# First scans of a Mamba and attention kernel: delta-times-u loads moved to SyncE's queue, the u piece loaded later

## The chip, the cores and the metric

The kernel runs on one core of a Trainium2 chip. The metric is the device time of one execution in microseconds (us); lower is better. Times of the kernel before are the median of three runs; the profile is of one more execution of the same program. TensorE is PE in the profile, VectorE DVE, ScalarE ACT, GpSimd POOL and SyncE SP.

## What is computed

The input x has 4 images of 4096 tokens (64 by 64) with 128 channels. Layer 0 adds to x the sum of three selective scans (forward, backward, and over 16 interleaved slices) of the normalised image; layer 1 adds attention and then a layer of 64 experts. The change concerns the scans alone. For each of the three orders the reference does this, with 256 channels d and 16 states n:

```python
def step(h, inp):
    u_, de_, b_, c_ = inp
    dA = jnp.exp(de_[..., None] * A)
    h = h * dA + (de_ * u_)[..., None] * b_[:, None, :]
    y = jnp.einsum('bdn,bn->bd', h, c_)
    return (h, y)
...
y = y + Dp[None, :, None] * x      # x is u here
return y * silu(z)
```

u is a convolved and activated projection of the image, delta (de_ above) a softplus of a further projection, and b_ and c_ are rows of another projection (B and C in the kernel).

## The kernel before

**Inputs and scans.** Class Inputs makes u, delta, delta times u (called du), B and C for every image, order and chunk of 1024 tokens, and keeps them in HBM. Its matmuls are lines L416 (the convolution, cv), L431 (xd), L444 (dt) and L375 (the gate z); ScalarE activates their results (u L423, r L449, z L381) and issues the stores of u and delta at L400, of B and C at L435 and L436, and of the gate at L383. Class Scans runs the recurrences.

**A step of a scan.** One step handles 8 channels by 16 states, or rather half of the states of 16 channels, on 128 partitions and 1024 tokens: a tile of delta and a tile of du, each 16 rows spread over 8 partitions a row (512 KB written), serve two steps. There are 3 orders x 4 chunks x 32 steps = 384 steps for an image. The steps of a group of four give 32 channels of y. For image 0 (alone is true) a step is:

- ScalarE: dA = exp(delta times A), L546, in place for odd steps, into another tile for even ones;
- VectorE: dB = du times B into PSUM, L555, then the scan h, L565, which goes on from the column ends of the chunk before;
- GpSimd: the last column of h is kept in ends, L567, and hC = h times C, L572;
- TensorE: sums hC over states into y, L603, for two steps at a time, one group later; after the fourth step of a group it adds the D term at L608 as a matmul of a diagonal (ScalarE makes it at L613) with the piece of u;
- ScalarE copies y to o, L628; SyncE stores o two steps later, as one DMA (L641, order 0) or four (L648, L652, orders 1 and 2).

**Order of the work.** The order is written out by hand (manual_schedule): every engine does its instructions in the order in which the program names them, and a DMA is issued by the sequencer of the engine that it is called on, in that engine's order. In the first phase the loop of tile_kernel gives the generator of image 0's scans one turn and the generators of the inputs of all four images 1.4 turns, alternately; the scans' loop has two turns a step. So on ScalarE the exponentials stand between the activations of the inputs, and on TensorE the y matmuls between those of the inputs.

**Loads.** At the start of step s the loop calls load(s + ahead), where ahead is 4 for image 0. For even steps it loads delta (3 buffers, issued by SyncE) and du (4 buffers, issued by ScalarE when alone, otherwise by SyncE), both at L531. For the first step of a group it also loads the piece of u for the D term, 128 KB, at L536 (3 buffers, SyncE). At the first two steps of a chunk, load first brings rows of B and C (L512). The piece of u is read at L608, in the third step of the following group. After its loads, step s calls exp(s + 3), then the y matmuls of the turn, then step(s), which does the scan and the next dB.

Of the kernel before, what the change touches and what calls it, by code (L numbers as in the profile page):

```python
# [11 lines left out]
F32 = mybir.dt.float32  # L12
# [4 lines left out]
P = 128  # L17
# [9 lines left out]
T = 1024  # L27
NC = L // T
NS2 = NS // 2
# [182 lines left out]
def orders(b):  # L212

    return ORDERS[min(b, 1)]
# [253 lines left out]
class Scans:  # L468
# [24 lines left out]
    def of_image(self, b, made, alone=False):  # L493

        nc = self.nc
# [5 lines left out]
        steps = [(order, c, k, j) for order in orders(b) for c in range(NC) for k in range(8) for j in range(4)]  # L501
        spread, ends, tiles, stores = {}, {}, {}, []
        ahead = 2 * self.AHEAD if alone else self.AHEAD

        def rows_of(order, c, q):
            for i, name in enumerate(("B", "C")):
                if alone and 2 * (c % 2) + q == 3:
                    t = self.lone.tile([P, T], F32, tag=name, name=f"{name}{q}_{b}_{order}_{c}")
                else:
                    t = self.rows.tile([P, T], F32, tag=name, bufs=3, name=f"{name}{q}_{b}_{order}_{c}")  # L510
                src = made[b, order, c]["bc"][i, q * NS2 : (q + 1) * NS2]
                nc.sync.dma_start(out=t, in_=src.unsqueeze(0).to_broadcast([16, NS2, T]))  # L512
                spread[order, c, name, q] = t
            if q == 1:
                return
            if c < NC - 1:
                ends[order, c] = self.small.tile([P, NB], F32, tag="ends", name=f"ends_{b}_{order}_{c}")

        def load(s):

            order, c, k, j = steps[s]
            if k == 0 and j < 2:
                rows_of(order, c, j)
            if j % 2:
                return
            at = 8 * (4 * k + j)
            for name, bufs in (("delta", 3), ("du", 4)):
                t = self.deep.tile([P, T], F32, tag=name, bufs=bufs, name=f"{name}_{b}_{s}")
                src = made[b, order, c][name][at : at + 16]
                by = nc.scalar if alone and name == "du" else nc.sync  # L530
                by.dma_start(out=t, in_=src.unsqueeze(1).to_broadcast([16, NS2, T]))  # L531
                tiles[name, s] = tiles[name, s + 1] = t
            if j == 0:
                u = self.rows.tile([P, T // 4], F32, tag="u", bufs=3, name=f"us_{b}_{s}")
                src = made[b, order, c]["u"][32 * k : 32 * k + 32]
                nc.sync.dma_start(out=u, in_=src.rearrange("p (g t) -> g p t", g=4))  # L536
                tiles["u", s] = u

        def exp(s):
            order, c, k, j = steps[s]  # L540
            t = tiles["delta", s]
            if j % 2 == 0:
                tag, bufs = ("dB", 3) if alone else ("dA", 2)
                tiles["delta", s] = self.deep.tile([P, T], F32, tag=tag, bufs=bufs, name=f"dA_{b}_{s}")
            A = self.ws[order]["A"][:, j % 2, 2 * k + j // 2].unsqueeze(1)
            nc.scalar.activation(tiles["delta", s], t, AF.Exp, scale=A)  # L546
# [10 lines left out]
        def step(s):  # L557

            order, c, k, j = steps[s]
            at = 4 * k + j  # L560
            dA, dB = tiles.pop(("delta", s)), tiles["du", s]
            tag = "dA" if alone and j % 2 else "h"
            h = self.deep.tile([P, T], F32, tag=tag, bufs=2, name=f"h_{b}_{s}")
            first = 0.0 if c == 0 else ends[order, c - 1][:, at : at + 1]
            nc.vector.tensor_tensor_scan(h, dA, dB, first, ALU.mult, ALU.add)  # L565
            if c < NC - 1:
                nc.gpsimd.tensor_copy(ends[order, c][:, at : at + 1], h[:, T - 1 :])  # L567
            if alone:
                if s + 1 < n:
                    inputs(s + 1)  # L570
                tiles["du", s] = self.lone.tile([P, T], F32, tag="hC", bufs=6, name=f"hC_{b}_{s}")
                nc.gpsimd.tensor_mul(tiles["du", s], h, spread[order, c, "C", j % 2])  # L572
                return
            if s + 1 < n:
                inputs(s + 1)
            nc.vector.tensor_mul(dB, h, spread[order, c, "C", j % 2])  # L576
            product(s)
# [32 lines left out]
        def diagonal(s):  # L610
            order, c, k, j = steps[s]
            d = self.lone.tile([P, P], F32, tag="diagonal", name=f"diag_{b}_{s}")
            nc.scalar.mul(d, self.ident, self.ws[order]["D"][:, k : k + 1])  # L613
            tiles["D", s] = d
# [44 lines left out]
        def have(s):  # L659
            while (b,) + steps[s][:2] not in made:  # L660
                yield

        for s in range(ahead):
            yield from have(s)
            load(s)
# [10 lines left out]
        def sums(s):  # L676

            if s % 4 in (1, 2):
                first = s // 4 * 4 - 4 + (0 if s % 4 == 1 else 2)
                total(first, y)  # L680
                total(first + 1, y)

        def finish(s, y):
            out(s, y)
            self.bank.leave()

        for s in range(n):
            if s + ahead < n:
                yield from have(s + ahead)
            turn = s % 4 if s >= 4 else None  # L690
            if turn == 1:
                while not self.bank.free:
                    self.did.add("wait")
                    yield
                y = self.bank.grab(f"y_{b}_{s}")
                if alone:
                    diagonal(s - 2)
            if s + ahead < n:
                load(s + ahead)
            if s + further < n:  # L700
                exp(s + further)
                self.did.add("exp")
            if turn in (1, 2):
                sums(s)
                self.did.add("sum")
            yield
            step(s)
            if turn == 2 and not alone:
                finish(s - 3, y)
            if turn == 0 and alone and s >= 8:  # L710
                finish(s - 5, y)
            if turn == 2 and stores:
                stores.pop()()
            yield
            self.steps[b] += 1
# [975 lines left out]
```

## Time and profile before

| | |
|---|---|
| median of 3 runs | 11474.27 us (11466.94 to 11487.52) |
| the profiled execution, its own time | 11464.56 us |
| span of that execution, first to last instruction | 11462.8 us |
| TensorE busy, share of the span | 87% |
| ScalarE busy | 88% |
| VectorE busy | 72% |
| GpSimd busy | 33% |
| DMA from SyncE's queue | 1345.93 MB, 44.5% of 16 engines' time |
| DMA from ScalarE's queue | 233.46 MB, 6.7% |
| scans of image 0 | first scan at 108 us, last ends near 1863 us |
| between 90 and 1870 us | VectorE busy 1494.0 us, TensorE 1362.0, GpSimd 1304.6, ScalarE 1151.3; DMA 0.80 busy, 223 GB/s |

In the views, a line such as "L546 ACT ACTIVATE dA<-delta,A" names the line of the program, the engine, the operation and what it writes and reads. A row of waits reads: who waited, for whom, us in total, number of times, the longest. A row of the order of time reads: start, duration (both us), engine, line, operation, count, and in brackets the idle time before it with what ended it. "ACTq" and "SPq" are the sequencers of ScalarE and SyncE issuing DMAs. In the name delta<-d_delta, d_ marks the tensor in HBM.

### The profile page before, as it was taken

How to read it: one execution, taken by the hardware profiler on the slowest of the kernel's cores; microseconds unless marked ns; L12 is line 12 of the kernel's file. 1: busy time of each engine (PE TensorE's matmuls, PEld its weight loads, DVE VectorE, ACT ScalarE, POOL GpSimd, SP SyncE). 2: the span in 40 equal slices, each digit the busy share in tenths (PEclk: the TensorE clock that was granted, in tenths of full speed). 3: DMA queues.
4: the chain of work that ended last, by engine and by line, in shares of the span. 5: the costliest groups of instructions: out<-in, count | busy, mean ns of one | idle time of the engine just before them, and what ended most of it. 6: DMA issues, size and time to landing. Idle time of an engine off the chain costs nothing.

```text
span 11462.8 us, 183364 instructions
## 1 busy us (share of the span) xinstructions
PE 9939.9 (87%) x68550; PEld 3315.0 (29%) x68550; DVE 8234.0 (72%) x8300; ACT 10070.4 (88%) x11032; POOL 3749.5 (33%) x3891
## 2 busy tenths in 40 slices
PE   6687783688998889999998898999998999999995
PEld 2233332222222222222222222222222223333323
DVE  6988877788888987999888979988998321111212
ACT  4666663799999999999999999999999999989992
POOL 5867764332323312424333224233332110000000
PEclk9888886899999999999999999999999999999997
DMA  6877877555565665655556656655556332222225
GB/s 196 237 228 219 221 206 211 159 149 148 148 160 151 168 176 155 160 149 149 147 145 157 195 154 156 160 141 147 150 146 168 118 98 71 74 73 83 75 65 185
DMA packets 900979, 1747.52 MB, mean 152 GB/s; under 512 B 203150, under 2 KB 443846, under 8 KB 899830
## 3 DMA queue, kind: packets, MB, share of 16 engines
q1 hardware_dynamic: 731198, 1345.93, 44.5%
q10 hardware_dynamic: 75032, 233.46, 6.7%
q0 software_dynamic: 93856, 156.41, 4.8%
q8 instruction: 538, 8.81, 0.3%
q14 instruction: 355, 2.91, 0.1%
HBM read 1379.76 MB, written 355.47 MB: 151 GB/s over the span
## 4 chain that ended last, share of the span: by engine, by line
PE 39%; ACT 25%; issue 14%; DVE 11%; DMA 7%; POOL 2%; SPq 1%; ACTq 1%; DVEq 0%; POOLq 0%
PE acc L1031 21%; ACT e L1022 20%; PE s L1017 10%; DVE h L565 5%; PE cv L416 4%; DMA delta<-d_delta 2%; DMA du<-d_du 2%; DVE dB L555 1%; ACT dA L546 1%; PE y L603 1%; POOL hC L572 1%; ACT delta L546 1%; PE fo L1188 1%; PE h L1175 1%; POOL ends L567 1%
## 5 line engine op out<-in xcount | busy, mean ns | idle before, releaser
L1022 ACT ACTIVATE e<-s 128x1024 f32<-128x1024 f32 x8192 | 7779.8, 1107 | 235.6 <-PE s L1017 219.7
L1031 PE MATMUL acc<-e,val 128*32 128x512 f32 x32768 | 5248.4, 615 | 105.8 <-ACT av L1040 92.7
L1017 PE MATMUL s<-qm,key 32*128 32x512 f32 x16384 | 2650.9, 501 | 591.2 <-ACT e L1022 561.3
L1017 PEld LDWEIGHTS s<-qm,key 32*128 32x128 f32 x16384 | 1012.7, 184 | 4449.5 <-issue 2485.0
L567 POOL COPY ends<-h 128x1 f32<-128x1 f32 x1152 | 1277.0, 1111 | 2352.7 <-DVE h L565 2338.6
L555 DVE TENSOR_TENSOR dB<-du,B 128x1024 f32<-128x1024 f32 x960 | 1231.8, 1283 | 484.5 <-DMA du<-d_du 251.1
L565 DVE TENSOR_TENSOR_SCAN h<-dA,ends,dB 128x1024 f32<-128x1024 f32 x576 | 1350.3, 2344 | 142.7 <-ACT dA L546 102.3
L1031 PEld LDWEIGHTS acc<-e,val 128*32 128x32 f32 x32768 | 970.2, 109 | 1605.1 <-issue 785.7
L546 ACT ACTIVATE dA<-delta,A 128x1024 f32<-128x1024 f32 x768 | 936.1, 1219 | 275.3 <-DMA delta<-d_delta 244.6
L565 DVE TENSOR_TENSOR_SCAN h<-delta,ends,du 128x1024 f32<-128x1024 f32 x432 | 1012.3, 2343 | 128.2 <-ACT delta L546 64.1
L572 POOL TENSOR_TENSOR hC<-h,C 128x1024 f32<-128x1024 f32 x384 | 1008.2, 2626 | 257.8 <-PE y L603 187.3
L546 ACT ACTIVATE delta<-delta,A 128x1024 f32<-128x1024 f32 x768 | 938.2, 1222 | 56.6 <-issue 22.3
L576 DVE TENSOR_TENSOR du<-h,C 128x1024 f32<-128x1024 f32 x576 | 701.1, 1217 | 0.1
L576 DVE TENSOR_TENSOR dB<-h,C 128x1024 f32<-128x1024 f32 x576 | 701.0, 1217 | 0.0
L555 DVE TENSOR_TENSOR du<-du,B 128x1024 f32<-128x1024 f32 x576 | 690.5, 1199 | 3.7 <-DMA B<-d_bc 3.7
L1046 POOL DMA_DIRECT2D d_ctx<-av x512 | 261.2, 520 | 1019.5 <-DVE av L1040 644.3
L416 PE MATMUL cv<-xn,conv 128*128 128x512 f32 x1024 | 478.9, 623 | 22.4 <-ACT xn L349 14.1
L597 POOL DMA_DIRECT2D d_du<-x_delta x272 | 157.7, 580 | 1003.0 <-DVE x_delta L596 940.8
L565 DVE TENSOR_TENSOR_SCAN h<-dA,dB 128x1024 f32<-128x1024 f32 x192 | 438.7, 2285 | 60.7 <-ACT dA L546 46.7
L603 PE MATMUL y<-hC,sel 128*32 128x256 f32 x3072 | 259.7, 472 | 248.1 <-issue 100.4
L603 PE MATMUL y<-dB,sel 128*32 128x256 f32 x4608 | 377.1, 399 | 9.7 <-DVE xT L1215 5.4
L565 DVE TENSOR_TENSOR_SCAN h<-delta,ends,dB 128x1024 f32<-128x1024 f32 x144 | 337.6, 2344 | 58.2 <-ACT delta L546 44.2
(252 smaller groups left out, 7338.1 us busy)
## 6 DMA issues: line engine op xcount, KB each, us to landing
delta<-d_delta SPq DMA_DIRECT2D x768, 512.0 KB
du<-d_du SPq DMA_DIRECT2D x576, 512.0 KB
du<-d_du ACTq DMA_DIRECT2D x192, 512.0 KB
key<-d_q SPq DMA_DIRECT2D x352, 256.0 KB
d_u<-u ACTq DMA_DIRECT2D x48, 1024.0 KB
d_delta<-r ACTq DMA_DIRECT2D x48, 1024.0 KB
B<-d_bc SPq DMA_DIRECT2D x96, 512.0 KB
C<-d_bc SPq DMA_DIRECT2D x96, 512.0 KB
```

Source lines behind the costliest of these rows:

```text
L416: nc.tensor.matmul(banks[2 * m + g], w["conv"][:, k, m * P : (m + 1) * P], reads(k, g), start=(k == 0), stop=(k == 3))
L546: nc.scalar.activation(tiles["delta", s], t, AF.Exp, scale=A)
L555: nc.vector.tensor_mul(tiles["du", s], du, spread[order, c, "B", j % 2])
L565: nc.vector.tensor_tensor_scan(h, dA, dB, first, ALU.mult, ALU.add)
L567: nc.gpsimd.tensor_copy(ends[order, c][:, at : at + 1], h[:, T - 1 :])
L572: nc.gpsimd.tensor_mul(tiles["du", s], h, spread[order, c, "C", j % 2])
L576: nc.vector.tensor_mul(dB, h, spread[order, c, "C", j % 2])
L603: nc.tensor.matmul(y[32 * g : 32 * g + 32, : T // 4], self.sel[:, j // 2, :], hC[:, 256 * g : 256 * g + 256], start=(j == 0), stop=(j == 3 ...
L1017: nc.tensor.matmul(s_ps[:, k, :], keys[f"{i // 4}"][rows, cut].bitcast(F32R), queries[j, qb][rows, :].bitcast(F32R), start=True, stop=True,)
L1022: nc.scalar.activation(e, s_ps, AF.Exp, scale=1.0 / math.sqrt(D))
L1031: nc.tensor.matmul(accs[j, qb][32 * k : 32 * k + 32, :], v[:, k * VW : k * VW + 32], es[i][k // 2][:, k % 2, :], start=(kc == 0), stop=(kc ...
L1046: nc.gpsimd.dma_start(out=self.context[b][h * D : h * D + D, cut], in_=av[32 * k : 32 * k + D, :])
```

## The change

For image 0, the loads of du are issued by SyncE, directly after those of delta. The piece of u is no longer loaded with the loads of the first step of its group, four steps ahead; a function of its own, bring_u, loads it in the second step of its own group, after that step's loads. For the other images the piece is loaded where it was. The loads themselves, their shapes and the numbers of buffers are the same.

```diff
             for name, bufs in (("delta", 3), ("du", 4)):
                 t = self.deep.tile([P, T], F32, tag=name, bufs=bufs, name=f"{name}_{b}_{s}")
                 src = made[b, order, c][name][at : at + 16]
-                by = nc.scalar if alone and name == "du" else nc.sync
-                by.dma_start(out=t, in_=src.unsqueeze(1).to_broadcast([16, NS2, T]))
+                nc.sync.dma_start(out=t, in_=src.unsqueeze(1).to_broadcast([16, NS2, T]))
                 tiles[name, s] = tiles[name, s + 1] = t
-            if j == 0:
-                u = self.rows.tile([P, T // 4], F32, tag="u", bufs=3, name=f"us_{b}_{s}")
-                src = made[b, order, c]["u"][32 * k : 32 * k + 32]
-                nc.sync.dma_start(out=u, in_=src.rearrange("p (g t) -> g p t", g=4))
-                tiles["u", s] = u
+            if j == 0 and not alone:
+                bring_u(s)
+
+        def bring_u(s):
+            order, c, k, j = steps[s]
+            u = self.rows.tile([P, T // 4], F32, tag="u", bufs=3, name=f"us_{b}_{s}")
+            src = made[b, order, c]["u"][32 * k : 32 * k + 32]
+            nc.sync.dma_start(out=u, in_=src.rearrange("p (g t) -> g p t", g=4))
+            tiles["u", s] = u
...
             if s + ahead < n:
                 load(s + ahead)
+            if alone and s % 4 == 1:
+                bring_u(s - 1)
             if s + further < n:
                 exp(s + further)
                 self.did.add("exp")
```

## The prediction

> **What bounds the kernel now.** The page was read first for where the time lies (span 11462.8 us; the chain gives TensorE 39% and ScalarE 25%, nearly all of it in the attention loop after 2200 us). The change touches only the scans of image 0, so the second view is the table of stretches, one for each chunk of 32 steps. Columns: stretch, length, busy time (and instructions) of TensorE, its weight loads, VectorE, ScalarE, GpSimd, then granted clock, DMA share, GB/s.
>
> ```profile
> core 0: us, PE busy (x) PEld busy (x) DVE busy (x) ACT busy (x) POOL busy (x), PEclk, DMA share, GB/s
> 382.00:515.00 133.00, 92.48 (x446) 38.46 (x444) 124.55 (x74) 81.80 (x102) 118.45 (x67) 0.86 0.92 265
> 652.00:811.00 159.00, 136.65 (x512) 54.13 (x511) 121.65 (x64) 114.79 (x135) 106.04 (x66) 0.88 0.75 223
> 811.00:962.00 151.00, 117.53 (x522) 50.14 (x520) 121.84 (x71) 98.89 (x125) 107.90 (x66) 0.87 0.82 227
> 1566.00:1733.00 167.00, 153.34 (x562) 62.69 (x560) 124.53 (x66) 114.78 (x139) 104.50 (x64) 0.90 0.78 213
> ```
>
> VectorE needs 120 to 125 us for a chunk; the first four take 133 to 137, the later ones up to 167. So VectorE sets the pace of the early chunks, and later something makes it wait. The third view is VectorE's list of waits from 90 to 1870 us (total, times, longest), with the one row of SyncE's list and the group row for its multiply in the same stretch:
>
> ```profile
> DVE dB L555 <- DMA du<-d_du: 83.3, 45, 7.3
> DVE h L565 <- ACT dA L546: 62.5, 20, 10.6
> DVE h L565 <- ACT delta L546: 52.0, 28, 4.9
> ```
>
> ```profile
> SPq L536 <- PE y L608: 219.7, 54, 10.4
> ```
>
> ```profile
> L555 DVE TENSOR_TENSOR dB<-du,B 128x1024 f32<-128x1024 f32 x384 | 536.4, 1397 | 95.2 <-DMA du<-d_du 83.3 <-DMA B<-d_bc 0.3
> ```
>
> VectorE waits 83 us for du and 114 us for ScalarE's exponentials. The multiply's mean is 1397 ns where an unhindered one takes 1233: 384 x 0.164 = 63 us more. The fourth view, the order of time around one such wait, says why du is late:
>
> ```profile
> 1485.03 0.51 SPq L531 DMA_DIRECT2D delta<-d_delta  x1
> ```
>
> ```profile
> 1486.71 2.42 ACT L449 ACTIVATE r<-dt,dt_proj_b 128x512 f32<-128x512 f32 x4
> 1489.16 0.38 ACTq L400 DMA_DIRECT2D d_delta<-r  x1
> ...
> 1495.65 2.06 ACT L381 ACTIVATE z<-z 128x512 f32<-128x512 f32 x4
> 1497.75 0.38 ACTq L383 DMA_DIRECT2D d_sz<-z  x1
> 1498.22 0.71 ACTq L531 DMA_DIRECT2D du<-d_du  x1
> ```
>
> ```profile
> 1508.14 1.23 DVE L555 TENSOR_TENSOR dB<-du,B 128x1024 f32<-128x1024 f32 x1 [4.24 <-DMA du<-d_du]
> ```
>
> delta and du of step 310 belong together; SyncE issued delta at 1485.03, ScalarE came to du at 1498.22, 13.2 us later, behind its activations and behind a 1 MB store in its own queue. Pairing all 192 issues in order, du is issued a median of 6.7 us after its delta, over 10 us in 60 of them, and earlier in 28.
>
> **What the Trainium skill says.** "DMA: Bandwidth & Descriptors", section Issuing engines are not separate DMA queues: DMAs of all issuing engines run on the same 16 engines and interleave, so a second issuer saves only issue time. The trace agrees that engines are shared: from 1019 to 1024 us ScalarE's queue moved 1.54 MB and SyncE's 0.00, though a delta was issued at 1020.0. The same page, section Anatomy of one DMA: a wait stands at the issuing sequencer, ahead of dispatch. The trace agrees: the du above was not even issued. "SBUF — State Buffer", section SBUF: two separate sides: VectorE with two SBUF inputs and a GpSimd op that reads SBUF exclude each other for a whole instruction. The trace fits: after a du wait the multiply often takes 2.4 to 3.4 us, as if it waited out a 2.35 us hC of GpSimd.
>
> **The change, part by part.**
> 1. *du issued on SyncE (192 issues).* A new delta's buffer is released by the scan five steps before its own; SyncE issues it 0.03 us after that scan ends in three cases of four. du follows 0.55 us later (one issue is 0.53). It needs no other buffer wait: its buffer was last read three steps earlier than delta's. From there to its multiply are four steps of 3.75 us (1497.80 to 1501.55, scan to scan), less the 0.55: 14.4 us. Two loads of 0.52 MB at the 223 GB/s of this stretch are 4.7 us, after some 1.5 us in which nothing moves yet (a delta issued at 1005.02 found the engines idle; bytes move from 1006.5). In all 44 du waits after the first step, du had been issued 4.5 to 14.5 us before the multiply, delta 16.4 to 26.7 us. I take these waits as gone: 76.2 us, and the 33.8 us by which the multiplies right after them were stretched: 110.0 us freed on VectorE.
> 2. *What of this is kept.* ScalarE's exponentials are next late. I count a freed wait as kept only as far as ScalarE, before the next scan that waited for an exponential, itself waited for delta or for VectorE; there it moves along. That leaves 69.5 of the 110.0: 41.8 in the eight chunks where TensorE is busy under 80%, 27.7 in the four (652, 1109, 1406 and 1566 us on) where it is busy 85 to 92%. In those I keep a third, 9, since cv matmuls hold ScalarE (168 us of waits in 69 places) and, through y, GpSimd (187 us in 57). Kept: 51 us. Bounds: 17.5 (the first four chunks alone, where no exponential is late) and 110.
> 3. *ScalarE rid of the issues.* 192 x 0.57 us = 109 us of its in-order time. Counting only issues that lie between ScalarE's last wait of any kind and a late exponential, and no more than that wait's length, 24.6 us of 119 us come free; most of it is in the four full chunks, so I take half, 12. Bounds 0 and 38 (the sum when waits for TensorE are not counted as breaks).
> 4. *SyncE gains 192 x 0.53 = 102 us of issuing.* Its work per four steps of 15 us is then four loads, one u and up to four stores, under 5 us. The cover is its own waiting for scans (666 us in its list). It passes the stores of o, which wait for ScalarE, and B and C loads: du is now held behind these as delta already is; delta was held up 78.6 us in 31 places, 7.7 at most, against 14.4 us of room. Nothing on average, up to the price in the third rival.
> 5. *The u piece.* Moved from ten steps before its D matmul to five; SyncE's 219.7 us of waiting for that matmul goes, because the buffer of three groups earlier has then long been read. It stood behind delta in front of the next load, which waits for a scan anyway, so I count nothing; bound: part of those 78.6 us. The new lead is some 17 us (four steps, and hC's 2.35) against 1.5 + 5 us to land behind delta and du (1.18 MB), 11.5 if a store holds the engines 5 us. At the 11 chunk starts, behind B and C, I charge 0.5 us each: 5 us.
>
> Sum: 51 + 12 - 5 = 58 us. The profiled execution took 11464.6 us (span and 1.8 around it), so 11406.6; the median of before is 11474.3, 9.7 above it, so **11416** for a median. Image 0's result is what attention waits for, and nothing after 1900 us is changed, so what the scans gain the end gains.
>
> **The rivals.**
> *TensorE and GpSimd take over the waits.* Over 650 to 1100 us the chain gives PE cv 32.9%, GpSimd's hC and ends 19.8% and du only 2.4%; GpSimd needs 2.35 + 1.24 us a step, nearly VectorE's 3.75, and cannot catch up. Then only the 17.5 us of the early chunks remain: 11457. Against it: du waits also lie where TensorE is under 80% busy.
> *All of it is kept:* 110 + 38 = 148 us, 11326, should exponentials move along, since delta no longer shares the engines with a du from the other queue. ScalarE waits 174 us for delta. Against it: the full chunks.
> *SyncE's queue as a single file (slower).* At a chunk start it gets B, C, delta, du twice within 8 us: eight loads, 4.2 MB. At 223 GB/s a load is 2.35 us, so the first du lands 9.4 + 1.5 us after the first load is issued, 9.3 after its own issue, and the second 10.9 us after its own. If ScalarE's d_u and d_delta, 2.1 MB, take the engines first, as one did at 1019, at that stretch's 310 GB/s for 6.8 us, these become 16.1 and 17.7, past the 14.4 us of room from which it decides. Price: 1.7 + 3.3 us late and twice 2.4 of stretch, 9.8 us, at 11 starts 108; less the 58 gained elsewhere: 50 slower, 11524. Against it: the bytes are the same as before on the same engines, and the stretch with 265 GB/s has hardly a wait.
>
> **Chances.** Forecast 0.50 (its own range 11385 to 11448), takeover 0.18, all kept 0.20, single file 0.12. About 0.2%, 23 us, is what a measurement can tell from no change. Faster 0.70, same 0.18, slower 0.12. The range 11330 to 11485 leaves out just under half of "all kept" and most of "single file".
>
> **What would show it.** Right: du rows of SyncE 0.5 us behind delta's; VectorE's du waits under 20 us; the multiply's mean near 1300 ns; SyncE's L536 row gone; ScalarE's row in VectorE's waits not above 150 us; last scan near 1805 us. Wrong: exponential or GpSimd waits grow by what du's lost, or du waits gather at chunk starts.

## The result, and the profile after

The changed kernel takes 11448.0 us (median of 11 runs, 11436.9 to 11458.3) against 11476.9 (11 runs, 11466.9 to 11491.0): a ratio of 0.9973 with an interval of 0.9963 to 0.9982, or 29 us less. The forecast was 58.

The profiled execution took 11451.7 us (span 11450.0). The last scan of image 0 ends at 1835 us instead of 1863, and the first score matmul of attention starts at 2078 instead of 2106. These 28 us agree with the 29 between the medians. The two profiled spans differ by 12.8 only: what follows the last scan is the same work in both, and took 9600 us in the one execution and 9615 in the other (9596 to 9619 in e1 to e3 below). The runs of one kernel spread over 21 to 24 us.

First the table of stretches, one for each chunk of 32 steps, as before (stretch, length, busy time of TensorE, its weight loads, VectorE, ScalarE, GpSimd, clock, DMA share, GB/s):

```profile
core 0: us, PE busy (x) PEld busy (x) DVE busy (x) ACT busy (x) POOL busy (x), PEclk, DMA share, GB/s
373.00:505.00 132.00, 95.64 (x462) 40.14 (x451) 126.23 (x75) 83.77 (x105) 118.99 (x67) 0.85 0.89 263
643.00:794.00 151.00, 133.23 (x515) 53.79 (x514) 117.58 (x64) 114.56 (x135) 110.48 (x66) 0.92 0.78 235
794.00:943.00 149.00, 114.39 (x523) 49.40 (x521) 126.84 (x70) 99.22 (x125) 110.69 (x67) 0.89 0.83 230
1540.00:1697.00 157.00, 143.89 (x538) 59.05 (x537) 125.74 (x65) 112.88 (x137) 105.68 (x63) 0.92 0.77 218
```

The same four chunks took 133, 159, 151 and 167 us; the first four together went from 544 to 538 us, the last eight from 1211 to 1191. So most of the gain lies in the late chunks. Each of these figures is of one execution: e2 below, as fast as the kernel before, took 550 and 1221, so differences of up to some 10 us between such figures show nothing. Next VectorE's waits from 90 to 1870 us, the row of its multiply there, and SyncE's longest wait:

```profile
DVE h L568 <- ACT dA L549: 81.8, 26, 10.9
DVE h L568 <- ACT delta L549: 59.0, 24, 6.4
DVE dB L558 <- DMA du<-d_du: 30.7, 4, 14.9
```

```profile
L558 DVE TENSOR_TENSOR dB<-du,B 128x1024 f32<-128x1024 f32 x385 | 551.8, 1433 | 43.8 <-DMA du<-d_du 30.7
```

```profile
SPq L530 <- DVE h L568: 737.0, 153, 11.1
```

Of the du waits of 83 us, 31 are left, and these are at the start of the scans (13.6), at one place in the fourth chunk (2.3), and for the next image's first load at the end of the stretch. The waits for exponentials went from 114 to 141 us, and the multiply's mean did not fall (1433 ns against 1397). SyncE's row for the D matmul is gone. In order of time, du now follows at once:

```profile
744.02 0.53 SPq L530 DMA_DIRECT2D delta<-d_delta  x1
744.60 0.59 SPq L530 DMA_DIRECT2D du<-d_du  x1
```

Over the whole stretch of the scans, idle time ahead of VectorE's multiplies fell from 95.2 to 28.9 us, idle time ahead of its scans rose from 156.5 to 184.9, and the time that the multiplies took beyond 1233 ns each, their stretch, was 77.3 us instead of 63.1. That is 66.3 - 28.4 - 14.2 = 23.7 us less, which is nearly all of the 26 by which the stretch from first to last scan got shorter (1755 to 1729); the first scan starts 3 us earlier.

### The profile page after: what moved, and what is told of

Read it like the earlier page. It is cut to its first block, busy times and chain, and to the rows that moved or that the text cites. A ratio compares the mean times of both kernels' runs of the same rounds, so it can differ in the third digit from the quotient of the medians.

```text
span 11450.0 us, 183259 instructions
## 1 busy us (share of the span) xinstructions
PE 9934.4 (87%) x68550; PEld 3314.2 (29%) x68550; DVE 8250.0 (72%) x8300; ACT 10073.1 (88%) x11032; POOL 3796.1 (33%) x3891
## 4 chain that ended last, share of the span: by engine, by line
PE 40%; ACT 24%; issue 14%; DVE 12%; DMA 8%; POOL 2%; SPq 1%; ACTq 0%; DVEq 0%; POOLq 0%
PE acc L1036 20%; ACT e L1027 20%; PE s L1022 10%; DVE h L568 5%; PE cv L416 4%; DMA delta<-d_delta 3%; DVE dB L558 2%; DMA du<-d_du 1%; PE y L606 1%; ACT dA L549 1%; ACT delta L549 1%; PE fo L1193 1%; POOL hC L575 1%; PE h L1180 1%; DMA w<-in_L_ffn_weight_dram 1%
## 5 line engine op out<-in xcount | busy, mean ns | idle before, releaser
L570 POOL COPY ends<-h 128x1 f32<-128x1 f32 x1152 | 1333.9, 1159 | 2246.9 <-DVE h L568 2235.4
L579 DVE TENSOR_TENSOR du<-h,C 128x1024 f32<-128x1024 f32 x576 | 701.6, 1218 | 0.1
L579 DVE TENSOR_TENSOR dB<-h,C 128x1024 f32<-128x1024 f32 x576 | 701.4, 1218 | 0.0
```

## The experiments

Two theories stood against each other after this. One: du's earlier issue made the gain, and part of it was lost to exponentials that are next late, as the prediction had it. Two: ScalarE, rid of 192 issues, made the gain, and du's earlier issue was worth little.

**Each half alone.** e1 is the change without the u half, e2 the u half alone.

```diff
 e1 (against the changed kernel)
-            if j == 0 and not alone:
+            if j == 0:
                 bring_u(s)
...
-            if alone and s % 4 == 1:
-                bring_u(s - 1)
 e2
-                nc.sync.dma_start(out=t, in_=src.unsqueeze(1).to_broadcast([16, NS2, T]))
+                by = nc.scalar if alone and name == "du" else nc.sync
+                by.dma_start(out=t, in_=src.unsqueeze(1).to_broadcast([16, NS2, T]))
```

> Only the du half of the change: du on SyncE behind delta, the u piece still loaded in the first step, four steps ahead. Theory (the gain is du's earlier issue; SyncE's wait for the u piece falls in time in which it waits for scans anyway): as the whole change, 11448 +- 10 us, VectorE's du waits under 30 us from 90 to 1870 us. Rival (the u piece's wait of 220 us would hold du and the next delta up): 11470 or more, du waits over 50 us or delta held up well over 68 us in all.

> Only the u half: the u piece loaded in its group's second step, du still issued by ScalarE. Theory (no part of the gain): 11477 +- 10 us, SyncE's row of waits for the D matmul gone, VectorE's du waits about 80 us. Rival (the u half carries a good part of it): 11460 or less.

e1 took 11452.3 us, a ratio of 0.9972 (0.9960 to 0.9983); e2 11480.0, 1.0000 (0.9991 to 1.0008). The du half is the whole change. In e1 SyncE still waited 206 us for the D matmul, and delta was held up by 100 us in all instead of 68, without a cost that can be measured. Most of the 206 us falls in time in which SyncE would otherwise wait for a scan: its wait for scans is 557 us there and 737 in the changed kernel.

**du early, but ScalarE still issues.** e3 leaves du on SyncE and puts a small DMA at each old place.

```diff
                 tiles[name, s] = tiles[name, s + 1] = t
+                if alone and name == "du":
+                    bit = self.lone.tile([P, 16], F32, tag="bit", bufs=2, name=f"bit_{b}_{s}")
+                    nc.scalar.dma_start(out=bit, in_=src.unsqueeze(1).to_broadcast([16, NS2, T])[:, :, :16])
```

> The whole change, and ScalarE still issues 192 DMAs at the places of the old du issues, but small ones (64 bytes on each of 128 partitions, into a tile that nobody reads). It tells ScalarE's freed time from du's earlier issue. Prediction's step 3 (12 us): 11460. If the freed time is worth nothing: 11448. If it is all of the gain: 11477, with VectorE's du waits still small.

It took 11481.2 us, a ratio of 1.0003 (0.9994 to 1.0011): the gain is gone. The row of the small DMAs shows that an issue costs ScalarE what the old one did (min, median, max ns), and VectorE's waits from 90 to 1870 us show where the du waits went:

```profile
L534 ACTq DMA_DIRECT2D bit<-d_du x192: 521/522/1989, 95.7 to 1853.4; - x192
```

```profile
DVE h L571 <- ACT dA L552: 88.8, 27, 10.5
DVE h L571 <- ACT delta L552: 76.6, 37, 8.0
...
DVE dB L561 <- DMA du<-d_du: 10.3, 3, 4.8
```

du waits are 10 us instead of 83, exponential waits 165 instead of 114. Most of what VectorE no longer waits for du, it waits for exponentials. The 192 small transfers add traffic of their own (64 bytes a partition), so e3 alone could overstate the case; its counterpart was needed.

**ScalarE freed, but du late.** e11 issues du on SyncE two steps behind delta, e13 does so only from step 128 on.

```diff
-            for name, bufs in (("delta", 3), ("du", 4)):
+            for name, bufs in (("delta", 3), ("du", 4))[: 1 if alone and s >= ahead else 2]:
...
+            if alone and s % 2 == 0 and ahead <= s + 2 < n:
+                bring_du(s + 2)
 e13: 128 in both places instead of ahead
```

> The counterpart of e3: the whole change, but SyncE issues du two steps (7.5 us) later than delta, about the median lag of before, so that ScalarE is rid of the issues and du is late all the same. If ScalarE's freed time is the whole gain: 11448 to 11458, although VectorE's du waits are 50 us or more again. If du's early issue were needed for it: 11470 or more. The prediction's own parts (51 for the waits, 12 for ScalarE) would give 11465.

> As e11, but du is issued two steps late on SyncE only from step 128 (the fifth chunk) on, where du was 8.9 us behind delta before too; in the first four chunks it follows delta at once. e11 had the whole gain in its last eight chunks and lost as much in its first four. If ScalarE's freed time alone makes the gain there: 11448 to 11458, the last eight chunks 1191 +- 10 us with VectorE's du waits over 40 us in them. If du's early issue is needed: 11470 or more.

e11 took 11475.2 us, 1.0001 (0.9993 to 1.0010), which looked like "du's early issue is needed". By chunks it is not so: its last eight took 1192 us, as the changed kernel's 1191, and its first four 566 instead of 538. In these du came 8.8 us behind delta (median), where the kernel before had it at 3.5, so e11 had made du later than it was there. e13, made to settle this, took 11441.4 us, 0.9972 (0.9962 to 0.9983): the whole gain, its last eight chunks 1188 us, though du came a median of 9.3 us behind delta in them (8.9 before). VectorE's waits of e13 from 660 to 1830 us:

```profile
DVE dB L566 <- DMA du<-d_du: 45.0, 25, 4.5
DVE h L576 <- ACT dA L557: 44.8, 15, 7.3
DVE h L576 <- ACT delta L557: 42.3, 20, 5.6
```

The same stretch in the changed kernel (it has no row for du), and in the kernel before:

```profile
DVE h L568 <- ACT dA L549: 81.8, 26, 10.9
DVE h L568 <- ACT delta L549: 55.3, 22, 6.4
```

```profile
DVE dB L555 <- DMA du<-d_du: 68.0, 38, 6.1
DVE h L565 <- ACT dA L546: 62.5, 20, 10.6
DVE h L565 <- ACT delta L546: 50.3, 27, 4.9
```

In this stretch the changed kernel waits 0 us for du and 137 for exponentials, e13 45 and 87, together nearly the same; the kernel before 68 and 113. The sum fell with ScalarE's freed time, and only its split depends on when du is issued. The profiled executions side by side, for the last eight chunks, in us (du behind delta is the median from one issue to the other; e3's issues on ScalarE are the small ones):

| | 192 issues on ScalarE | du behind delta | waits for du | waits for exponentials | last eight chunks |
|---|---|---|---|---|---|
| before | yes | 8.9 | 68 | 115 | 1211 |
| e2 | yes | 9.2 | 69 | 101 | 1221 |
| e3 | yes | 0.6 | 0 | 161 | 1218 |
| changed | no | 0.6 | 0 | 140 | 1191 |
| e1 | no | 0.6 | 0 | 154 | 1192 |
| e11 | no | 9.4 | 54 | 86 | 1192 |
| e13 | no | 9.3 | 45 | 87 | 1188 |

The length goes with ScalarE's issues, and not with when du is issued. Theory two holds for these chunks. For the first four, du as late as it was in the kernel before with ScalarE freed was not run.

**What stretches the multiply.** e7 replaces GpSimd's hC by writes that read no SBUF.

```diff
-                nc.gpsimd.tensor_mul(tiles["du", s], h, spread[order, c, "C", j % 2])
+                for cut in (slice(0, T), slice(0, T), slice(0, T // 2)):
+                    nc.gpsimd.memset(tiles["du", s][:, cut], 0.0)
```

> The whole change with hC not computed in image 0's scans: GpSimd writes zeros there instead, in two and a half writes of about the same 2.3 us, and so reads no SBUF; y there is the D term alone. If VectorE's multiply is stretched by a GpSimd operation that reads SBUF, its mean falls from 1433 ns to under 1260 and the 77 us of stretch to under 10; the last scan ends 40 us or more earlier. If the stretch has another cause, the mean stays over 1380 ns.

One run: 11404.3 us, last scan 1817. VectorE's multiply:

```profile
L558 DVE TENSOR_TENSOR dB<-du,B 128x1024 f32<-128x1024 f32 x385 | 474.6, 1233 | 40.1 <-DMA du<-d_du 27.0
```

Not one is stretched any more, so the stretch does come from hC, the GpSimd multiply that reads SBUF beside it. The stretch of 77 us is gone, but the scans end only 18 us earlier: the waits for exponentials grew from 141 to 215 us. This is the same exchange as with du. It shows in the chunks: 66 of the 77 us lay in the last eight, and these took 1192 us as in the changed kernel (1191); the first four, where VectorE hardly waits for an exponential, took 519 instead of 538.

What brings hC beside the multiply is for the most part GpSimd's wait for TensorE, which frees the buffers of hC with its y matmuls. GpSimd's row of waits for it from 90 to 1870 us, in the kernel before and in the changed one:

```profile
POOL hC L572 <- PE y L603: 187.3, 57, 7.3
POOL hC L575 <- PE y L606: 244.1, 71, 9.3
```

In the changed kernel 59 multiplies take over 1.5 us. Of these, 56 start during an hC that stands in a run of GpSimd work without idle time, and this run began when a wait for y ended; in the kernel before it is 35 of 48.

**Is it TensorE that holds ScalarE?** e5 is the kernel before, e6 the changed one, both with two of four convolution taps left out.

```diff
-                for k in range(4):
+                for k in range(2):
...
-start=(k == 0), stop=(k == 3)
+start=(k == 0), stop=(k == 1)
```

> The kernel before with two of the four taps of the convolution (half of the cv matmuls, L416) left out, in all images. If TensorE's cv holds ScalarE and GpSimd: last scan of image 0 ends 60 to 120 us earlier than 1863, and ScalarE's wait for cv falls from 168 to under 60 us. If it does not: under 30 us earlier.

> The changed kernel with the same two taps left out; to be set against e5_before_half. If the freed du waits are lost only because TensorE's cv is next late (the prediction's step 2), the change is now worth 55 to 110 us. If the change is worth ScalarE's freed time alone, it stays at 20 to 35 us.

In e5 the scans end at 1762 us instead of 1863, so TensorE's convolution does hold them up. e5 took 11371.0 us and e6 11322.6; against the kernel before 0.9910 (0.9897 to 0.9924) and 0.9867 (0.9854 to 0.9881). The change is worth 48 us here, not 29: between the two ranges given for e6. In e5 ScalarE's wait for cv is 29 us instead of 168:

```profile
ACT u L423 <- PE cv L416: 29.1, 22, 2.7
```

VectorE waits 21 us for exponentials and 103 for du in e5, 63 and 30 in e6. With half of the cv matmuls gone, 73 us less for du bring 42 more for exponentials, so more of the du waits may be kept; how much of the 48 is that, and how much ScalarE's freed time, was not separated.

**u's activation one step later.** e9 adds two turns between the cv matmuls and ScalarE's activation of u in the changed kernel; e14 also gives the inputs 1.5 turns instead of 1.4; e15 makes both edits in the kernel before.

```diff
                 yield
         yield
+        yield
+        yield
         for m in range(2):
...
-                others.run(1.4)
+                others.run(1.5)
```

> The changed kernel with ScalarE's activation of u placed two turns (one step) later behind its cv matmuls, so that ScalarE waits less for TensorE in front of the exponentials. If those waits (192 us of ScalarE for cv) make the exponentials late: the wait falls under 80 us, VectorE's waits for exponentials from 141 to under 110, and the time to 11425 or less. If ScalarE is late by its own work: 11448 +- 10.

> The changed kernel with u's activation one step later (e9), and the inputs of the other images given 1.5 turns for each turn of the scans instead of 1.4, since in e9 the scans ended 120 us earlier but the inputs 105 us later. If the wait of ScalarE for TensorE is what is left: the two end together near 1770 us, 11385 +- 20 us. If the inputs alone set the end of the phase: 11440 or more.

> The kernel before with the same two edits as e14; set against it, it gives what the change under study is worth where ScalarE waits less for TensorE. With half of the convolution left out it was worth 48 us, on the kernel as it is 29. Expected here: between the two, so 11425 +- 20. If the change's worth hung on ScalarE's waiting: under 15 us apart.

e9 took 11450.5 us, 0.9977 (0.9969 to 0.9986), no faster than the changed kernel, and yet its scans end at 1715 us instead of 1835, with 61 us of waits for exponentials and 109 us of ScalarE's waits for cv instead of 192. The gain stood behind another wait:

```profile
DVE a_half_pi L56 <- ACT r L451: 131.0, 1, 131.0
```

The inputs of the other images now ended at 1846 us instead of 1741, and the next phase waits for them. The two turns thus have a second effect: they make every piece of the inputs longer in turns, so that less of the inputs runs beside the scans. When the scans of e9 ended, 1361 of the 1536 cv matmuls had been started, in the changed kernel all of them. How much of the 120 us comes from the later activation and how much from the slower inputs was not separated. e14 brings the two streams nearer (scans 1776, inputs 1823) and took 11430.7 us, 0.9964 (0.9951 to 0.9978), well short of the 11385 expected; e15 took 11456.0, 0.9989 (0.9983 to 0.9996). The change is worth 25 us between these two: about what it was without the edits, and not between 29 and 48 as expected. e14 has the lowest ratio to the kernel before of all that compute the whole result, but its interval overlaps that of the changed kernel, so a further gain is not shown.

**More issues taken from ScalarE.** e12 moves the stores of u, delta, B and C to SyncE too.

```diff
-            nc.scalar.dma_start(out=made[name].rearrange("(m p) t -> p m t", p=P), in_=t)
+            nc.sync.dma_start(out=made[name].rearrange("(m p) t -> p m t", p=P), in_=t)
...
-        nc.scalar.dma_start(out=made["bc"][0], in_=xd[B_ROW : B_ROW + NS])
+        nc.sync.dma_start(out=made["bc"][0], in_=xd[B_ROW : B_ROW + NS])
```

> The changed kernel, and the stores of u, delta, B and C (188 issues, L400, L435, L436) go from ScalarE to SyncE too. If ScalarE's in-order time is what counts, 192 freed issues gave 29 us, so these give about 25: 11425. If SyncE, which must then wait for ScalarE's results ahead of the loads, is held up: 11460 or more, and delta is issued late far more than the 68 us of the changed kernel.

It took 11595.1 us, 1.0108 (1.0094 to 1.0122), 125 us slower than the kernel before. SyncE's waits and VectorE's from 90 to 1870 us:

```profile
SPq L400 <- ACT u L423: 380.9, 39, 19.5
SPq L400 <- ACT r L449: 197.7, 33, 11.0
```

```profile
DVE dB L558 <- DMA du<-d_du: 258.5, 81, 13.8
```

SyncE stands in front of a store until ScalarE has its result, and the loads stand behind it: delta was held up by 1683 us in 156 places, against 68 in 32. ScalarE, with fewer issues, waited 65 us for cv instead of 192, but 494 us for delta instead of 194.

## Why the prediction was right in direction and twice too large

The sum of 58 us was twice the 29 measured, and its two main terms were wrong in opposite ways: 51 us were put on what gave nothing that can be measured, and 12 on what gave the whole gain. The direction was right because of the small term; that the sum came no further off is luck. The result, 11448.0, lies at the end of the forecast's own range (11385 to 11448) and nearer to the takeover's 11457 than to 11416.

1. *du issued on SyncE.* Right as to the waits: from the second step on 76 us became 2. Wrong as to the stretch: I took the 33.8 us after those waits as freed with them, but the whole stretch did not fall (77 us against 63, and 85 in e2, where the du waits are as before). e7 shows that its cause is GpSimd's hC, as the prediction had it; but most of the multiplies that it meets hang on GpSimd's waits for y, and these remained.
2. *What of this is kept.* This is the step that failed: 51 us were to be kept, and e3, where du's early issue stands alone, gained nothing. There du's waits fell by 73 us and those for exponentials grew by 51. The rule was too mild: it asked if ScalarE had anywhere waited for delta or VectorE before the next late exponential. That ScalarE's own work between two such waits was still as long as before, and so became late as VectorE got ahead, is my reading; it fits the length of the last eight chunks, which follows ScalarE's issues alone.
3. *ScalarE rid of the issues.* Put at 12 us with bounds of 0 and 38; it is the 29 of the whole change (e13 has all of it with du late from the fifth chunk on, e3 none of it with du early). The term was halved because TensorE fills four chunks, and it counted only waits for exponentials; but a du issued late was ScalarE's lateness as well.
4. *SyncE's extra issues* and 5. *the u piece.* Nothing, as forecast, by e1 and e2; delta's hold-ups went from 80 to 68 us. The 5 us charged at chunk starts are too small to be seen.

Of the signs named, du's rows 0.57 us behind delta's, the end of SyncE's L536 row and waits for exponentials under 150 us (141) came; a multiply's mean near 1300 ns and a last scan near 1805 us did not.

Of the rivals, the takeover has the mechanism that took the gain, though the change itself shows only part of its sign: du's waits lost 53 us and those for exponentials grew by 26 (51 for 73 in e3). GpSimd's part in it is not a wait of VectorE, which waits 7 us for hC, 3 before; it is the stretch, and e7 shows that in the last eight chunks the end would not have come earlier without it. The single file did not occur in the change itself, and e12 shows the form in which it is real: loads behind stores that wait for ScalarE, not loads behind loads. What stays open is why 109 us of ScalarE's freed in-order time give 29; e5 and e6 show that TensorE's cv matmuls have a part in it, without giving the share, and e9 fits this but slows the inputs too.

## What to carry to other kernels

When one consumer waits in turn for two suppliers that the same engine holds up, here VectorE for du and for exponentials, take their waits as one sum: here, removing the one handed most of its time to the other, until the engine itself had less to do. A DMA that an engine issues is in-order time of that engine, and is best given to a sequencer that has to wait for nothing of that engine. A phase that ends with the later of two streams gains only when both get shorter, so look at the end of the other stream before shortening one.

## What the runs showed of the hardware

VectorE's multiply of two SBUF tensors into PSUM takes 1.23 us, up to 3.43 us in the changed kernel (3.36 before) beside a GpSimd multiply that reads SBUF, and 1.23 us every time in e7, beside GpSimd writes that read none. The Trainium skill has the rule in "SBUF — State Buffer", section SBUF: two separate sides: a VectorE operation with two SBUF inputs and a GpSimd operation that reads SBUF shut each other out for a whole instruction. e7 agrees with it. A load issue of 128 partitions by 64 bytes holds ScalarE as long as one of 128 by 4096: 522 ns in both.
